# A two-layer vision network with selective scans, 16 images on one core: the order of instructions written by hand in place of a scheduler's

## The chip, the cores and the metric

The kernel runs on one core of a Trainium2 chip. The metric is the time of one execution on the device, in microseconds (us); less is better. The core has a matrix engine (PE, with its weight loads shown apart as PEld), a vector engine (DVE), an activation engine (ACT), a general engine (POOL), and SP, which here only issues DMAs. Each takes the instructions of its own queue in the order in which the program holds them; between engines they wait on semaphores.

## The reference, cut to what matters

Sixteen images of 48 x 48 pixels and 96 channels pass through two layers. Each layer adds a convolution-and-scan block and then a feed-forward block. The scan block is what costs:

```python
xz = x @ in_proj_w.T; xc, z = split(xz)             # 192 channels each
xc = silu(depthwise_conv3x3(xc))
xs = 4 directions of xc                             # rows, columns, both reversed
dts, B, C = split(x_proj(xs))                       # 6 + 16 + 16 per direction
delta = softplus(dt_proj(dts) + bias)
h = h * exp(delta * A) + (delta * u) * B            # 2304 pixels, 192 channels, 16 states
y = sum over states of h * C                        # + Ds * xs
y = merge of the 4 directions, then * silu(z)
out = y @ out_proj_w.T
```

The first layer also has a branch on y: a product to 384 channels, a 3 x 3 depthwise convolution, a product to 96, scaled by a squeeze-and-excite factor. The second normalizes y over its channels ahead of the gate. The feed-forward block multiplies values rounded to 8-bit floats and rounds sums to 16 bits.

## The kernel before, in words

**Scan steps.** One image and layer is 288 scan steps (`STEPS`): two pairs of directions, three chunks of 768 pixels (`CH`), three groups j of 128 channel-direction rows, four parts i of 32 channels, four groups g of 4 states. The 128 partitions are 32 channels x 4 states. A step is: ACT computes `a = exp(d * rate)` into one of two PSUM buffers (line 484); POOL multiplies `b = du * B` (line 486); DVE runs the recurrence along the pixels (`tensor_tensor_scan`, line 518); the result is multiplied by C into `hc` (line 520), by DVE in place of `a` for three steps of four, and by POOL from a buffer of its own `h` for the fourth (`SHARE`); ACT copies the last column as carry for the next chunk (line 522); PE sums the 4 states with a constant matrix into the PSUM tile `py` (the fold, line 524, two products of 384 columns). `py` starts with the skip term or the first pair's result (line 504), and after 16 steps ACT copies it out (line 533) and it is stored (line 534). There are four buffers of `b` and of `hc`, four of `d` (delta and delta*u, a DMA for every four steps, line 466) and six of `bc` (B and C, four DMAs for every 24 steps, line 475).

**The other work** is written as generators that yield weights: `first` (norm, projection, convolution, and the inputs of the scan of layer 0), `middle` (all between the scan of layer 0 and that of layer 1 of one image: merge of directions, gate, `branch`, out-projection, feed-forward, then `before` for layer 1) and `final` (merge, `centred`, gate, out-projection, feed-forward). `conv` (line 324) makes a depthwise convolution of nine products by diagonal matrices per 384 pixels (line 333). Products go to two PSUM buffers (`pst`) and are evicted by ACT or DVE. `before` ends with the dt stage: for six column blocks, products (line 430), an eviction with bias (line 431), a softplus over 2304 pixels (line 435), and three products `du` on POOL (line 442).

**Phases.** `together` (line 781) runs one scan, 288 steps, and lets the other image's generators go on by weight, so that they end at 94% of the scan (`AHEAD`). For images in pairs the phases are: layer 0 of m beside `final(m-1)` and `first(m+1)`; layer 0 of m+1 beside `middle(m)`; layer 1 of m beside `middle(m+1)`; layer 1 of m+1 beside `final(m)` and `first(m+2)`. That is 32 phases. `first(0)` runs ahead of them and `final(15)` behind.

**What sets the order.** The program is traced in this order, but the framework's scheduler then orders each engine's instructions by priority and by buffers that come free. So the order on an engine isn't quite that of the text: the built program has, for instance, two scans ahead of two products in many places, and merges that start earlier than written. DMAs are issued by SP (loads, `du`) and by ACT (`y`, `u`, `dd`, `bc`, `xt` stores).

Of the kernel before, what the change touches and what calls it, by code (L numbers as in the profile page):

```python
# [13 lines left out]
BF16 = mybir.dt.bfloat16  # L14
F8 = mybir.dt.float8e5
AF = mybir.ActivationFunctionType
ALU = mybir.AluOpType
# [120 lines left out]
class Net:  # L138
    def __init__(self, ctx, tc, wpack, at, b2, ffw):
# [11 lines left out]
        self.xp = pool("xp", bufs=1)  # L151
        self.big = pool("big", bufs=5)
# [105 lines left out]
        self.turn = 0  # L258
# [12 lines left out]

    def norm(self, x, eps):

        nc = self.nc
        m = self.small.tile([128, NT], F32, name="m")
        nc.vector.tensor_reduce(m, x, AX.X, ALU.add)
        nc.vector.tensor_scalar_mul(m, m, 1.0 / DM)
        xm = self.bigt([128, NT, DM], "xm")
        nc.gpsimd.tensor_tensor(xm, x, m.unsqueeze(2).broadcast_to([128, NT, DM]), ALU.subtract)
        yield 6  # L280
        sq = self.bigt([128, NT, DM], "sq")
        nc.scalar.activation(sq, xm, AF.Square)
        s = self.small.tile([128, NT], F32, name="s")
        nc.vector.tensor_reduce(s, sq, AX.X, ALU.add)
        yield 2
        nc.scalar.activation(s, s, AF.Sqrt, bias=self.eps[eps], scale=1.0 / DM)
        r = self.small.tile([128, NT], F32, name="r")
        nc.vector.reciprocal(r, s)
        nc.gpsimd.tensor_tensor(xm, xm, r.unsqueeze(2).broadcast_to([128, NT, DM]), ALU.mult)
        yield 4  # L290
        return xm

    def channels_first(self, xn, dt, name):
# [3 lines left out]
        for q in range(NQ):  # L297
            p = self.pst()
            for i in range(TQ):
                nc.tensor.transpose(p[:DM, i * 128 : (i + 1) * 128], xn[:, TQ * q + i, :], self.ident)  # L300
            out = xt[:, q * SUB : (q + 1) * SUB]
# [4 lines left out]
            yield 1  # L306
# [17 lines left out]
    def conv(self, p, name, done):  # L324

        nc = self.nc
        dg = self.one.tile([128, 9, 128], F32, name="dg")
        nc.sync.dma_start(dg.rearrange("p k m -> p (k m)"), self.taps[name])
        for q in range(NQ):
# [10 lines left out]
            yield 6  # L340
            done(q, o)
            yield 0.8
# [3 lines left out]
    def before(self, t, s, x):  # L346
# [4 lines left out]
        nc.scalar.dma_start(s["xt"], xt)  # L351
        u = [None] * 3
        cb = self.get(t + "cb")
        for name, half in (("wxa", "a"), ("wxb", "b")):
            p = self.padded(name)
            for q in range(NQ):
                o = self.pst()
                nc.tensor.matmul(
                    o[:, :SUB], lhsT=self.get(t + name), rhs=xt[:, q * SUB : (q + 1) * SUB], start=True, stop=True
                )  # L360
                nc.scalar.copy(self.inside(p, q), img(o[:, :SUB]))
                yield 0.7
            if half == "a":
                u[0] = self.bigt([128, L], "u0")

                def done(q, o):
# [4 lines left out]
                yield from self.conv(p, t + half, done)  # L371
                nc.scalar.activation(u[0], u[0], AF.Silu)
                yield 1
                u[1] = self.bigt([128, L], "u1")
                nc.scalar.copy(swapped(u[1][64:]), img(u[0][64:]))
                yield 1
                u[2] = self.bigt([128, L], "u2")
                nc.scalar.copy(swapped(u[2][:64]), img(u[0][:64]))
                nc.scalar.dma_start(s["u"][0], u[0])
                yield 1  # L380
            else:

                def done(q, o):
# [10 lines left out]
                yield from self.conv(p, t + half, done)  # L394
                nc.scalar.activation(u[1][:64], u[1][:64], AF.Silu)  # L395
                nc.scalar.activation(u[2][64:], u[2][64:], AF.Silu)
                yield 1
                for j in (1, 2):
                    nc.scalar.dma_start(s["u"][j], u[j])
# [5 lines left out]
        for c in range(NCH):  # L405
            row = self.work.tile([128, CH], F32, name="row", tag="w3")
            for q in range(2):
                cs = slice(c * CH + q * SUB, c * CH + (q + 1) * SUB)
                for w, m in ((wdt, 4 * DR), (wbc, 128)):
                    o = self.pst()  # L410
                    for j in range(3):
                        nc.tensor.matmul(  # L412
                            o[:m, :SUB], lhsT=w[:, j, :], rhs=u[j][:, cs], start=(j == 0), stop=(j == 2)
# [489 lines left out]
```

## Time and profile before

| | |
|---|---|
| median of 3 runs | 29325.72 us (29315.92 to 29372.79) |
| profiled execution | 29326.56 us |
| its span, first to last instruction | 29324.8 us |
| busy: PE, DVE, POOL, ACT | 82%, 80%, 79%, 48% |
| weight loads (PEld) | 43% |
| DMA | 150 GB/s mean, 4406 MB |
| mean granted PE clock | 0.898 |
| first scan starts | 203.1 us |
| last scan ends | 176.5 us before the end |

The page says for each group of instructions how long it was busy and what ended the idle time of its engine before it. The waits view sums the latter by pairs of waiter and releaser. The windows view gives each engine's busy time in chosen stretches. A PE that is shown busy isn't always at its peak, since matrix products are pipelined and their ends modelled; its granted clock is 1.00 or 0.50 at any time, and a mean in a stretch.

The scan lines in numbers: 9216 steps; the product on POOL (line 486) 1819 ns, the recurrence on DVE 1741 to 1813 ns, the product on DVE 947 ns, the exponential on ACT 906 ns.

### The profile page before, as it was taken

The page shows a single profiled execution, that of the slowest core. Times are in us where ns is not written, and L with a number is a line of the kernel's source. Part 1 is how long each engine was busy: PE and PEld are TensorE (multiplying, and loading weights), DVE is VectorE, ACT ScalarE, POOL GpSimd, SP SyncE. Part 2 cuts the span into 40 slices and gives each one's busy share as a digit, 9 for nine tenths or more (in the row PEclk, how much of TensorE's full clock was granted, in tenths as well). Part 3 has the DMA queues.
Part 4 walks back from the last instruction along what each step waited for, and adds up shares of the span by engine and source line. Part 5 has one row for each costly group of instructions (what it writes and reads, how often), then busy time and mean ns, then how long its engine had stood idle before and what let it go on. Part 6 is the DMA issues. An engine that isn't in the chain of part 4 may idle for free. (4 is left out here: it accounts for less than half of the span.)

```text
span 29324.8 us, 227106 instructions
## 1 busy us (share of the span) xinstructions
PE 24033.6 (82%) x68224; PEld 12726.8 (43%) x68224; DVE 23488.3 (80%) x18372; ACT 14074.7 (48%) x22093; POOL 23241.6 (79%) x13238
## 2 busy tenths in 40 slices
PE   7888878888788887888788887888778888788886
PEld 3444444444444444444444444444444444344443
DVE  6877888778887788877888778887788877888777
ACT  4454444544445454444444444444444444444443
POOL 6877788778887788877888778787787877877777
PEclk8988899989999899998999989999898998989988
DMA  4444444444444444444444444444444344443443
GB/s 155 153 156 152 146 148 155 154 151 149 148 152 154 154 152 148 148 156 149 159 143 151 151 149 160 144 148 153 150 164 145 141 154 150 162 148 143 150 156 109
DMA packets 1062581, 4406.37 MB, mean 150 GB/s; under 512 B 211936, under 2 KB 211936, under 8 KB 1030368
## 3 DMA queue, kind: packets, MB, share of 16 engines
q1 hardware_dynamic: 869792, 3757.78, 36.2%
q10 hardware_dynamic: 191552, 634.06, 5.5%
q8 instruction: 536, 8.78, 0.1%
q14 instruction: 701, 5.74, 0.1%
HBM read 3500.22 MB, written 891.22 MB: 150 GB/s over the span
## 5 line engine op out<-in xcount | busy, mean ns | idle before, releaser
L486 POOL TENSOR_TENSOR b<-d,bc 128x768 f32<-128x768 f32 x9216 | 16584.7, 1819 | 4084.2 <-DVE a L518 2783.7
L524 PE MATMUL py<-hc,fold_sb 128*128 128x384 f32 x36864 | 14564.0, 540 | 3265.9 <-DVE hc L520 1991.2
L524 PEld LDWEIGHTS py<-hc,fold_sb 128*128 128x128 f32 x36864 | 7359.8, 208 | 9807.3 <-DVE hc L520 3050.8
L484 ACT ACTIVATE a<-d,l_a 128x768 f32<-128x768 f32 x9216 | 8304.2, 906 | 5248.7 <-DVE h L518 2817.0
L518 DVE TENSOR_TENSOR_SCAN a<-a,carry,b 128x768 f32<-128x768 f32 x4608 | 8252.7, 1813 | 2037.9 <-ACT a L484 1438.6
L520 DVE TENSOR_TENSOR hc<-a,bc 128x768 f32<-128x768 f32 x6912 | 6427.8, 947 | 1034.1 <-PE py L524 873.5
L520 POOL TENSOR_TENSOR hc<-h,bc 128x768 f32<-128x768 f32 x2304 | 4187.6, 1818 | 1511.8 <-DVE h L518 1115.4
L518 DVE TENSOR_TENSOR_SCAN a<-a,b 128x768 f32<-128x768 f32 x2304 | 4002.9, 1755 | 1091.6 <-ACT a L484 612.1
L522 ACT COPY carry<-a 128x1 f32<-128x1 f32 x4608 | 725.2, 158 | 5229.7 <-DVE hc L520 5210.7
L518 DVE TENSOR_TENSOR_SCAN h<-a,carry,b 128x768 f32<-128x768 f32 x1536 | 2766.9, 1801 | 484.0 <-ACT a L484 354.4
L333 PE MATMUL pst<-e,dg 128*128 128x384 f32 x5184 | 1730.3, 486 | 0.0
L430 PE MATMUL pst<-dts,wpack_sb 24*128 24x384 f32 x2304 | 1200.8, 636 | 513.9 <-ACT dl L431 434.2
L518 DVE TENSOR_TENSOR_SCAN h<-a,b 128x768 f32<-128x768 f32 x768 | 1337.2, 1741 | 303.9 <-POOL b L486 236.0
L333 PEld LDWEIGHTS pst<-e,dg 128*128 128x128 f32 x5184 | 977.2, 189 | 705.5 <-PE py L524 25.5
L333 PE MATMUL pst<-wxa,dg 128*128 128x384 f32 x3456 | 1173.3, 492 | 24.9 <-DMA dg<-taps_l0a 20.0
L442 POOL TENSOR_TENSOR du<-dl,u 128x768 f32<-128x768 f32 x576 | 1033.6, 1809 | 201.2 <-DMA dd<-du 100.4
L333 PE MATMUL pst<-wxb,dg 128*128 128x384 f32 x3456 | 1169.7, 489 | 5.6 <-issue 5.6
L431 ACT ACTIVATE dl<-pst,wpack_sb 128x384 f32<-128x384 f32 x1152 | 644.0, 577 | 1072.5 <-PE pst L430 581.4
L430 PEld LDWEIGHTS pst<-dts,wpack_sb 24*128 24x128 f32 x2304 | 446.7, 223 | 1206.6 <-ACT dl L431 661.4
L504 PE MATMUL py<-first,ident 128*128 128x384 f32 x1152 | 570.7, 629 | 484.5 <-ACT yt L533 479.6
L412 PE MATMUL pst<-u,wpack_sb 128*24 128x384 f32 (+1 forms) x2304 | 831.7, 492 | 65.2 <-ACT u L395 23.0
L333 PEld LDWEIGHTS pst<-wxa,dg 128*128 128x128 f32 x3456 | 661.5, 192 | 509.4 <-issue 44.6
(143 smaller groups left out, 15283.5 us busy)
## 6 DMA issues: line engine op xcount, KB each, us to landing
d<-dd SPq DMA_DIRECT2D x2304, 768.0 KB, 4.6
bc<-bc SPq DMA_DIRECT2D x1536, 768.0 KB, 6.0
dd<-dl ACTq DMA_DIRECT2D x192, 1152.0 KB, 4.7
dd<-du SPq DMA_DIRECT2D x576, 384.0 KB, 2.5
y<-yt ACTq DMA_DIRECT2D x576, 384.0 KB, 3.1
u<-u ACTq DMA_DIRECT2D x96, 1152.0 KB, 5.1
first<-u SPq DMA_DIRECT2D x288, 384.0 KB, 3.3
first<-y SPq DMA_DIRECT2D x288, 384.0 KB, 3.1
```

The costliest lines, as they stand in the source:

```text
L333: nc.tensor.matmul(img(o[:, :SUB]), lhsT=dg[:, k, :], rhs=img(p, PW)[:, PQ * q + i : PQ * q + i + PQ, j : j + HW], start=(k == 0), stop=(k ...
L412: nc.tensor.matmul(o[:m, :SUB], lhsT=w[:, j, :], rhs=u[j][:, cs], start=(j == 0), stop=(j == 2))
L430: nc.tensor.matmul(o[:, :SUB], lhsT=dtw[:, col, :], rhs=dts[:, cs], start=True, stop=True)
L431: nc.scalar.activation(dl[:, cs], o[:, :SUB], AF.Identity, bias=self.get(t + "dtb")[:, col : col + 1])
L442: nc.gpsimd.tensor_tensor(du, dl[:, cs], u[j][:, cs], ALU.mult)
L484: nc.scalar.activation(a, d[:, 0, :], AF.Exp, scale=rates[:, pair, j, i, g : g + 1])
L486: nc.gpsimd.tensor_tensor(b, d[:, 1, :], bc[:, 0, :], ALU.mult)
L504: nc.tensor.matmul(py[:, q, :SUB], lhsT=self.skip[t][:, j, :] if pair == 0 else self.ident, rhs=first[:, q * SUB : (q + 1) * SUB], start=True,
L518: nc.vector.tensor_tensor_scan(way(h), way(a), way(b), start, ALU.mult, ALU.add)
L520: (nc.vector if here else nc.gpsimd).tensor_tensor(hc, h, cc, ALU.mult)
L522: nc.scalar.copy(carry[:, at : at + 1], h[:, last : last + 1])
L524: nc.tensor.matmul(py[:, q, :SUB], lhsT=self.fold[:, i, :], rhs=hc[:, q * SUB : (q + 1) * SUB], start=False, stop=((i, g) == (3, GROUPS - 1)),
```

## The change

The whole traced part is put into `manual_schedule`, so each engine takes its instructions in the order of the text, and the text is rewritten for that:

- All 32 scans become one loop over 9216 steps (`scans`). In turn n it writes: due loads of `bc` and `d` (three tiles of four steps ahead); the recurrence of step n, the product on DVE if it is DVE's, the carry copy; the exponential of step n+2; POOL's product b of step n+3; POOL's product hc of step n, if it is POOL's; the fold of step n-1 (of n-2, if POOL made its hc); then pieces of the other work.
- The other work is cut into smaller pieces. `piped` runs products and their evictions as stages, an eviction one piece behind its product; `columns` and `conv` use it. Whole-image POOL instructions of norms and merges are split into thirds, and large ACT instructions are followed by larger yields.
- Weights are set anew: 320, 720 and 244 for `first`, `middle` and `final`, in place of 201, 464 and 151; the other work ends after 268 of 288 steps. In a `middle` phase the weights of the parts are 25 for the merge, 47 gate, 189 branch, 20 squeeze, 32 out-projection, 91 feed-forward, 46 norm and turn, 118 projection and convolution, 26 x-projection, 126 dt stage; in `final` 25, 39.4 (`centred`), 47, 42, 91.
- All stores go from ACT's queue to SP's. The pool of large buffers has six in place of five and now holds the tokens `xs`, the branch's `tm` (whole image) and the feed-forward's 8-bit tile.

The work itself, in count and size of instructions, is otherwise the same. The diff, cut to its core:

```diff
+    def piped(self, n, weight, *stages):
+        vals = [None] * n
+        for t in range(n + len(stages) - 1):
+            for k in reversed(range(len(stages))):
+                q = t - k
+                if 0 <= q < n:
+                    r = stages[k](q, vals[q])
+                    if inspect.isgenerator(r):
+                        r = yield from r
+                    vals[q] = r
+            yield weight if t < n else 1
...
-    def conv(self, p, name, done):
...
+    def conv(self, p, dg, put):
+        nc = self.nc
+        def nine(q, _):
             o = self.pst()
             for k in range(9):
...
-            yield 6
-            done(q, o)
-            yield 0.8
+                if k in (1, 3, 5):
+                    yield 1.5
+            return o
+        yield from self.piped(NQ, 2, nine, put)
...
+        def inputs(pair, j, dl):
+            to = s["dd"][pair, j].rearrange("p (c w f) -> p c w f", c=NCH, w=2)
+            nc.sync.dma_start(to[:, :, 0, :], dl.rearrange("p (c f) -> p c f", c=NCH))
+            for c in range(NCH):
+                du = self.work.tile([128, CH], F32, name="du", tag="w3")
+                cs = slice(c * CH, (c + 1) * CH)
+                nc.gpsimd.tensor_tensor(du, dl[:, cs], u[j][:, cs], ALU.mult)
+                nc.sync.dma_start(to[:, c, 1, :], du)
+                yield 2
...
+                yield from self.columns(1.5, put, (dtw[:, col, :], dts))
                 nc.scalar.activation(dl, dl, AF.Softplus)
-                to = s["dd"][pair, j].rearrange("p (c w f) -> p c w f", c=NCH, w=2)
-                nc.scalar.dma_start(to[:, :, 0, :], dl.rearrange("p (c f) -> p c f", c=NCH))
-                yield 1
...
+                yield 5
+                if done:
+                    yield from inputs(*done)
+                done = pair, j, dl
+        yield from inputs(*done)
...
+            if here:
+                product()
+                product = None
+            if c != (NCH - 1, 0)[pair]:
+                nc.scalar.copy(kept["carry"][:, at : at + 1], h[:, last : last + 1])
+            folds.append((n + (1 if here else 2), n, hc))
+            return product
...
+            for g, slot in enumerate((-16, -16, -3, -2)):
+                bc_at[block * 6 * GROUPS + slot if block else -16].append((block, g))
+        load_first(0)
+        for n in range(-4 * GROUPS, len(steps) + 3):
+            for block, g in bc_at.get(n, ()):
+                load_bc(block, g)
+            if n % GROUPS == 0 and 0 <= n // GROUPS + 3 < tiles:
+                load_d(n // GROUPS + 3)
+            product = step(n) if 0 <= n < len(steps) else None
+            if 0 <= n + 2 < len(steps):
+                decays(n + 2)
+            if 0 <= n + 3 < len(steps):
+                added(n + 3)
+            if product:
+                product()
+            while folds and folds[0][0] <= n:
+                _, m, hc = folds.popleft()
+                folded(m, hc)
+            if 0 <= n < len(steps):
+                f = n // STEPS
+                share = (n % STEPS + 1) / (AHEAD * STEPS)
+                while todo[f] is not None and (given[f] < total[f] * share or share >= 1):
+                    w = next(todo[f], None)
+                    if w is None:
+                        todo[f] = None
+                    else:
+                        given[f] += w
...
+        low = self.bigt([64, L], "low")
+        nc.scalar.copy(img(low), swapped(y[2][64:]))
+        yield 4
+        third = HW // 3
+        for into, of in ((img(y[0][:64]), swapped(y[2][:64])), (img(y[0][64:]), swapped(y[1][64:]))):
+            for i in range(3):
+                at = slice(i * third, (i + 1) * third)
+                nc.gpsimd.tensor_tensor(into[:, at], into[:, at], of[:, at], ALU.add)
+                yield 2
...
-WORK = {"first": 201, "middle": 464, "final": 151}
-AHEAD = 0.94
+WORK = {"first": 320, "middle": 720, "final": 244}
+AHEAD = 268 / 288
...
+    with tc.manual_schedule():
+        for _ in first(0)[0]:
+            pass
+        net.scans(phases)
+        for _ in final(NB - 1)[0]:
+            pass
```

## The prediction

> **What bounds the kernel now.** I read the page first, then cut the span at every 288th scan (line 518), since one phase of the program is 288 scan steps with the other image's work beside them. The columns of the two rows below: window, length, then busy time of PE, PE weight load, DVE, ACT, POOL (with instruction counts), granted PE clock, DMA share, GB/s. The first row is a phase with `middle` beside the scan, the second one with `final` and `first`.
>
> ```profile
> 11936.10:12876.20 940.10, 803.10 (x2290) 426.66 (x2289) 734.63 (x565) 450.59 (x706) 727.92 (x419) 0.90 0.41 147
> 13814.60:14694.40 879.80, 696.21 (x1981) 369.40 (x1980) 732.58 (x581) 429.62 (x675) 725.01 (x410) 0.90 0.44 156
> ```
>
> DVE and POOL are each 78% busy in the first and 83% in the second: three engines carry nearly the same load and none is full on average. Phases of one kind repeat within a few us: 16 with `middle` at about 938, 14 of the other kind at about 880, the first phase (only `first` beside it) 829.5, the last (only `final`) 782.8; 203.0 us lie ahead of the first scan and 176.5 behind the last. So the stage decides. I cut the `middle` phase where lines begin and end: merge and gate; branch convolutions; squeeze and out-projection; norms and feed-forward; the next layer's convolutions; x-projection (line 412); dt stage (lines 430 to 444); scan alone.
>
> ```profile
> 11936.10:12025.10 89.00, 66.86 (x169) 32.00 (x167) 64.44 (x49) 48.97 (x77) 81.83 (x46) 0.87 0.46 167
> 12025.10:12280.10 255.00, 253.81 (x772) 143.04 (x772) 212.96 (x164) 113.87 (x200) 195.68 (x116) 1.00 0.36 128
> 12280.10:12333.10 53.00, 49.97 (x183) 32.88 (x181) 42.63 (x37) 17.48 (x21) 33.79 (x20) 0.84 0.35 126
> 12333.10:12471.10 138.00, 92.22 (x288) 46.42 (x288) 121.53 (x107) 61.98 (x106) 110.72 (x68) 0.85 0.36 122
> 12471.10:12647.10 176.00, 153.17 (x450) 87.77 (x449) 130.19 (x95) 85.17 (x143) 122.33 (x71) 0.92 0.38 137
> 12647.10:12703.10 56.00, 49.93 (x144) 21.98 (x142) 40.04 (x30) 30.18 (x52) 35.81 (x20) 1.00 0.34 128
> 12703.10:12837.10 134.00, 110.13 (x228) 49.06 (x229) 87.29 (x64) 79.45 (x95) 108.81 (x62) 0.78 0.59 220
> 12837.10:12876.10 39.00, 26.90 (x65) 13.46 (x64) 35.44 (x26) 13.48 (x16) 38.84 (x20) 0.78 0.43 157
> ```
>
> The branch stage is PE-bound (253.8 of 255.0 us, clock 1.00); merge and gate are POOL-bound; feed-forward is DVE's; the dt stage has no full engine, its time is waits. Line 518 alone, over the same cuts, gives 28, 86, 15, 39, 55, 17, 37, 15 scans (one at a cut counts twice). The waits (waiter <- releaser: total us, times, longest) say who is late for DVE:
>
> ```profile
> DVE a L518 <- ACT a L484: 2050.8, 1411, 13.0
> DVE a L518 <- ACT carry L522: 905.8, 859, 11.3
> DVE hc L520 <- PE py L524: 873.5, 695, 5.7
> POOL b L486 <- DMA bc<-bc: 815.6, 471, 5.4
> ```
>
> ACT is 48% busy and yet it is the usual releaser: its exponentials stand behind evictions that wait for PE and behind long activations. The timeline of DVE near the last scans shows what a step costs there:
>
> ```profile
> 28901.04 1.75 DVE L518 TENSOR_TENSOR_SCAN a<-a,b 128x768 f32<-128x768 f32 x1
> 28902.90 0.96 DVE L520 TENSOR_TENSOR hc<-a,bc 128x768 f32<-128x768 f32 x1
> 28903.78 1.75 DVE L518 TENSOR_TENSOR_SCAN a<-a,b 128x768 f32<-128x768 f32 x1
> 28911.65 1.80 DVE L520 TENSOR_TENSOR hc<-a,bc 128x768 f32<-128x768 f32 x2
> 28913.81 1.82 DVE L518 TENSOR_TENSOR_SCAN a<-a,carry,b 128x768 f32<-128x768 f32 x1 [0.36 <-ACT carry L522]
> ```
>
> A product that follows its own scan starts 1.86 us after it; the next scan 0.88 later: 2.74 per pair. In the order scan, scan, product, product starts follow at some 1.7 and 0.86, but the exponential of the next step, which needs the product's PSUM buffer, then comes 0.36 late.
>
> **What the Trainium skill says.** "PSUM — Partial Sum Buffer", Engine vs sequencer instructions: ScalarE, VectorE and GpSimd queues are strict FIFO. The trace agrees: exponentials idle behind other lines' waits. "VectorE: DVE Perf Modes", The DRAIN you can't avoid: each DVE instruction waits for the pipe to empty, and a semaphore costs nothing extra. Here it does: 1.86 us from scan to dependent product, about 1.7 to an independent instruction; I use the trace. "ScalarE: Activation LUTs", What ACT_TABLE_LOAD costs: about 1283 ns; the trace has 1283 ns. "TensorE: Matmul & The Clock Gate", Part 1: the array runs at half or full clock, by recent activity. The trace agrees (granted clock 1.00 in the branch stage, 0.78 in the dt stage), so a denser PE needn't be priced at 0.90.
>
> **The change, part by part.** The instructions are the same but for small splits (norms in thirds, merge adds in parts), so what moves is order. The built order shows it: scan and product alternate, exponentials two steps ahead, POOL's product three, folds one or two behind.
>
> *Step cost on DVE.* Three steps of four become 2.74, the fourth (product on POOL) about 1.72: 9.94/4 = 2.48 us. The waits for the exponential go, since a pair lies between; after a POOL step only 1.7 lies between against 0.06 + 0.16 + 0.91 + 0.1 = 1.25 of carry copy and exponential, both from the trace. So 288 steps are 715 us, plus 30 to 40 of other DVE work. Light stretches gain little: line 518 alone has 81 scans in the 200 us from 28900, one at a cut counted twice: about 2.5 a step already.
>
> *Pacing.* New weights: `middle` is 720 over 268 steps, 2.69 a step, and 20 steps stay alone. Steps per stage are weight/2.69. PE takes 0.329 us per record (253.8/772), so 0.658 per 384-column product and 1.32 per step of folds. POOL takes 1.78 per instruction back to back (rows of four: 7.12), so 1.25 x 1.78 = 2.23 a step. Each stage takes the largest of the three:
> - merge and gate, 72 -> 26.8 steps: POOL 26.8 x 2.23 + 17.4 + 10.7 = 88, less 7 for its lead of three steps, plus 12 for waits. The `low` copy now stands on ACT ahead of later exponentials, behind fold 1.3, copy 0.8, y write 3.1 (its landing) and a load of 1152 KB (5.1, as u's): 93.
> - branch, 189 -> 70.3 steps: PE 216 x 0.658 + 70.3 x 1.32 + 6 = 240. Before it had 86 steps and 255 us: the convolution's share of weight falls from 44% to 28%, so it is squeezed into fewer steps.
> - squeeze and out-projection, 52 -> 19.4: 58.
> - norms and feed-forward, 137 -> 51: DVE 51 x 2.48 + 31 = 157.
> - next convolutions, 118 -> 43.9: 110 (PE, 30 steps) + 18 + 17 + 5 for SiLU and its table loads = 150.
> - x-projection, 26 -> 9.7: PE 23.7 + 12.8 = 36.5.
> - dt stage, 126 -> 46.9: POOL 46.9 x 2.23 + 18 x 1.78 = 137, less its lead, plus a few us of softplus with its two table loads (2.13 + 2.57): 140.
> - scan alone, 20: 49.5.
>
> Sum 924; plus 7 for bc loads whose buffer comes free three steps ahead of use (landing takes 6.0 us, two POOL products hide 3.6): 931 against 940, -9. Bounds: POOL's lead hides the bc and y waits, -20; none is hidden, +25.
>
> For `final` with `first` (564/268 = 2.1 a step) the same way: merge (POOL 11.9 x 2.23 + 17.4, +1), centring (DVE 18.7 x 2.48 + 6, +2) and gate (POOL 22.3 x 2.23 + 10.7, +3) 162; out-projections (20 steps) 58; feed-forward (43.2) 136; norm and turn (23.7) 65; convolutions (38 steps PE-bound at 121, 18 of DVE's at 44, +5) 170; x-projection (12.3) 40; dt stage (POOL 59.8 x 2.23 + 32, less a little lead) 164; alone 49.5. Sum 845, plus 7 for bc, plus 4 for the load of the tokens: 856 against 880, -24 (-45 to 0). The first phase (320/268) is DVE-bound: 715 + 10 + some 25 for ACT and POOL = 750, -80. The last: 715 + 45 + 11 = 771, -12.
>
> *Ahead and behind.* The written order puts the seven tap tables (DVE until 53 us) ahead of the first norm, which the scheduler began at 17.9, and the first scan behind all of `first`: from 203 to about 248, +45 (10 to 70). The tail is one image without scans in both: 0.
>
> *Buffers.* A sixth big buffer, with the tokens and the feed-forward's fp8 tile in it, changes no instruction; 476 us of ACT waiting for POOL's `du` (line 431 on 442) should go with it and is part of the dt stage above. *DMAs.* All issues of ACT's queue go to SP's (y, u, dd, bc, xt). ACT loses some 0.3 us each, on 960 issues, mostly in idle time: nothing counted. SP now waits in order for yt, rows and products; behind it stand d loads (12 steps ahead, 30 us: hidden) and bc loads (2 to 3 steps ahead: the 7 us above).
>
> Sum: 16 x -9 = -144; 14 x -24 = -336; -80; -12; +45: -527. The profiled execution has 29326.56 us, its span 29324.8, the median is 29325.72, one time for this purpose: 28,800 us, -1.8%.
>
> **Rivals.** *The waits hide too:* the DVE-bound and POOL-bound stages lose nothing beside their loads: 27 a `middle` phase and 25 the other kind less, 782: 28,020. For: the last scan-only stretches have DVE 95% busy. Against: softplus, SiLU and copies of 2 to 4 us hold the exponentials in any order. *PE falls short in the squeezed stretches (slower):* the folds and evictions share in-order queues with it, and the convolution stage of before had PE busy 153.2 of 176.0 us, 87%. PE-bound time after is some 440 us of a `middle` phase and 215 of the other; at 87% that is 66 and 32 more: 1500 in all, 30,300. It turns the sign once PE is busy below about 95% there (527/1500 of 13 points). For it: only two PSUM buffers for products. Against: the branch stage ran at 99.5%. *No change:* gains cancel within 0.2%, about what a measurement of this kernel can tell from none: 29,325. That the order isn't taken as written is excluded by the built order.
>
> **Chances.** Forecast 0.47 (own range 28,300 to 29,250), hidden waits 0.16, short PE 0.29, cancelled 0.08. Faster 0.63, same 0.08, slower 0.29. The range leaves out the best of the first rival and the worst of the second: 27,900 to 29,900.
>
> **What would show it.** Right: about 931 and 856 us a phase; PE near 99% and clock 1.00 in the branch stage at 3.4 us a step; scan to product at 1.86 throughout; DVE's waits for ACT down from some 3450 us to under 1500, those for PE up from 870; first scan near 250. Wrong: phases of both kinds below 850, or PE with idle time in the convolution stages while DVE waits for ACT.

## The result: slower by 2.4%, and the profile after

The median of four runs is 30049.29 us (30041.38 to 30060.83); four runs of the kernel before beside them have 29330.68 us. The ratio is 1.0243, with a 95% interval of 1.0225 to 1.0261. The profiled execution has a span of 30052.5 us, 727.7 more than before. Cut at every 288th scan (line 627 now), it falls into:

| | forecast, us | measured, us | difference to before, all |
|---|---|---|---|
| until the first scan | +45 | 260.1 (203.1) | +57 |
| first phase | -80 | 756.6 (829.3) | -73 |
| 16 `middle` phases, each | -9 | 974.6 (937.1) | +600 |
| 14 of the other kind, each | -24 | 890.7 (881.4) | +130 |
| last phase | -12 | 792.7 (782.8) | +10 |
| behind the last scan | 0 | 179.3 (176.5) | +3 |

The sign turns in the repeated phases. Here is the `middle` phase from 12201.0 us, cut as the one before was (window, length, busy time of PE, PE weight load, DVE, ACT, POOL, granted clock, DMA share, GB/s): merge and gate; branch convolutions; squeeze and out-projection; norms and feed-forward; next convolutions; x-projection; dt stage; scan alone.

```profile
12201.00:12301.90 100.90, 59.17 (x145) 29.09 (x146) 68.78 (x51) 46.61 (x76) 88.55 (x50) 0.80 0.45 163
12301.90:12537.40 235.50, 233.57 (x697) 128.82 (x697) 164.15 (x121) 93.47 (x178) 154.21 (x95) 0.99 0.32 113
12537.40:12614.50 77.10, 66.41 (x227) 39.89 (x226) 65.01 (x55) 26.33 (x32) 50.76 (x29) 0.87 0.32 105
12614.50:12787.00 172.50, 110.77 (x328) 56.60 (x327) 156.17 (x130) 71.45 (x115) 132.05 (x87) 0.81 0.33 117
12787.00:12938.00 151.00, 142.87 (x428) 81.17 (x426) 103.69 (x75) 77.66 (x125) 100.87 (x62) 0.98 0.36 129
12938.00:12981.00 43.00, 38.28 (x110) 17.37 (x110) 28.77 (x20) 21.31 (x40) 25.06 (x14) 0.96 0.44 165
12981.00:13129.00 148.00, 115.59 (x276) 55.62 (x275) 118.43 (x84) 92.89 (x124) 130.87 (x74) 0.85 0.61 213
13129.00:13175.20 46.20, 32.55 (x80) 16.79 (x80) 43.47 (x33) 16.09 (x18) 44.71 (x26) 0.85 0.50 183
```

Forecast were 93, 240, 58, 157, 150, 36.5, 140, 49.5. The two convolution stages (second and fifth line) came as forecast, PE 99% and 95% busy: 386.5 us against 390. They hold 66 and 43 scans; before they had 86 and 55 in 431 us. Some 32 steps were pushed out of the stages in which a step costs least (PE's four fold products, so (431 - 386.5)/32 = 1.39 us) into the others. Those took 587.7 us for 179 steps, before 509.1 for 147: 2.46 us for each step more. 32 x (2.46 - 1.39) = 34 us, which is the whole difference of these two phases (974.2 - 940.1). It must be, since both prices are differences divided by the same 32 steps; whether the squeeze is the cause, the first experiment asks. Put otherwise: at the 2.48 us of a bare step on DVE, the other stages hold 509.1 - 147 x 2.48 = 144.5 us beyond the scan before, and 587.7 - 179 x 2.48 = 143.8 after. At this price the written order took nothing off that. The forecast had (931 - 390) - 174 x 2.48 = 110.

The waits of after (waiter <- releaser: total us, times, longest) say why:

```profile
DVE a L627 <- ACT carry L637: 2504.8, 643, 14.5
...
ACT tm L743 <- PE pst L394: 1238.2, 288, 7.2
DVE a L627 <- ACT a L574: 857.3, 494, 5.9
...
ACT yt L612 <- PE py L603: 819.0, 283, 7.4
...
ACT u L429 <- PE pst L394: 719.3, 156, 28.7
```

The view says that the scans wait less for exponentials (857.3 us, before 2050.8) and more for the carry copy (2504.8, before 905.8). The names mislead here. A scan reads a carry of the chunk before, written 48 steps earlier; of ACT it needs only its own exponential. In the trace of after, the 762 scans that wait by name for the carry (`a` and `h` together) start 0.10 us behind the end of their own exponential, as the other 568 do; the carry copy merely ends in between. So both are one wait, for the exponential. Over all scans it was 3447 us in 2549 waits before, and is 3737 us in 1330 waits after: half as many, 2.8 us each in place of 1.35. ACT itself now stands for PE at every one of the 288 branch evictions (`tm`, 1238.2 us against 497.7). Over all lines ACT waits 5006 us for PE, before 3372. The timeline of ACT and DVE in the branch stage shows one such wait (start, length, engine, line, ..., idle time before it):

```profile
12329.54 1.75 DVE L627 TENSOR_TENSOR_SCAN a<-a,b 128x768 f32<-128x768 f32 x1
12331.62 0.96 DVE L631 TENSOR_TENSOR hc<-a,bc 128x768 f32<-128x768 f32 x1 [0.33 <-PE py L603]
12334.85 0.67 ACT L743 ACTIVATE tm<-pst,bn_b,bn_s 128x384 f32<-128x384 f32 x1 [7.24 <-PE pst L394]
12335.42 0.15 ACT L637 COPY carry<-a 128x1 f32<-128x1 f32 x1
12335.60 0.91 ACT L574 ACTIVATE a<-d,l_a 128x768 f32<-128x768 f32 x1
12336.44 0.15 ACT L637 COPY carry<-a 128x1 f32<-128x1 f32 x1
12336.60 1.77 DVE L627 TENSOR_TENSOR_SCAN a<-a,b 128x768 f32<-128x768 f32 x1 [4.03 <-ACT carry L637]
```

ACT stands 7.24 us at the eviction, until PE has the piece. The exponential at 12335.60 is that of the scan at 12336.60. Nothing on DVE holds it later than the first scan shown, but it stands behind the eviction, and so its scan stands 4.03 us. PE has work throughout: it isn't late by waiting, it is full.

### The profile page after: what moved, and what is told of

Its sections match the earlier page's. It is cut to its first block, busy times and chain, and to the rows that moved or that the text cites. A ratio compares the mean times of both kernels' runs of the same rounds, so it can differ in the third digit from the quotient of the medians.

```text
span 30052.5 us, 228448 instructions
## 1 busy us (share of the span) xinstructions
PE 23943.1 (80%) x68224; PEld 12686.2 (42%) x68224; DVE 23984.3 (80%) x18372; ACT 13991.5 (47%) x22020; POOL 23233.8 (77%) x13686
## 5 line engine op out<-in xcount | busy, mean ns | idle before, releaser
L580 POOL TENSOR_TENSOR b<-d,bc 128x768 f32<-128x768 f32 x9216 | 16542.7, 1812 | 3999.2 <-DVE a L627 3547.8
L603 PE MATMUL py<-hc,fold_sb 128*128 128x384 f32 x36864 | 15024.3, 550 | 4460.1 <-POOL hc L631 2229.8
L603 PEld LDWEIGHTS py<-hc,fold_sb 128*128 128x128 f32 x36864 | 7477.7, 212 | 11449.6 <-DVE hc L631 3263.9
L627 DVE TENSOR_TENSOR_SCAN a<-a,carry,b 128x768 f32<-128x768 f32 x4608 | 8359.8, 1814 | 1955.5 <-ACT carry L637 1158.3
L631 DVE TENSOR_TENSOR hc<-a,bc 128x768 f32<-128x768 f32 x6912 | 6622.0, 958 | 679.5 <-PE py L603 22.7
L627 DVE TENSOR_TENSOR_SCAN h<-a,carry,b 128x768 f32<-128x768 f32 x1536 | 2777.4, 1808 | 285.5 <-ACT carry L637 133.0
L295 PE MATMUL pst<-dts,wpack_sb 24*128 24x384 f32 x2304 | 1081.8, 581 | 192.5 <-ACT dl L505 191.3
L394 PEld LDWEIGHTS pst<-wxb,dg 128*128 128x128 f32 x3456 | 656.1, 190 | 464.8 <-issue 6.9
L612 ACT COPY yt<-py 128x768 f32<-128x768 f32 x576 | 457.7, 795 | 821.9 <-PE py L603 819.0
L295 PE MATMUL pst<-u,wpack_sb 128*128 128x384 f32 (+1 forms) x2304 | 816.3, 499 | 8.4 <-ACT u L458 4.5
```

The source lines that it names most:

```text
L295: nc.tensor.matmul(o[: w.shape[1], :SUB], lhsT=w, rhs=y[:, q * SUB : (q + 1) * SUB], start=(k == 0), stop=(k == len(terms) - 1),)
L394: nc.tensor.matmul(img(o[:, :SUB]), lhsT=dg[:, k, :], rhs=img(p, PW)[:, PQ * q + i : PQ * q + i + PQ, j : j + HW], start=(k == 0), stop=(k ...
L580: nc.gpsimd.tensor_tensor(b, d[:, 1, :], bc[:, 0, :], ALU.mult)
L603: nc.tensor.matmul(py[:, q, :SUB], lhsT=self.fold[:, i, :], rhs=hc[:, q * SUB : (q + 1) * SUB], start=False, stop=end,)
L612: nc.scalar.copy(sub(yt), py[:, :, :SUB])
L627: nc.vector.tensor_tensor_scan(way(h), way(a), way(b), start, ALU.mult, ALU.add)
```

## The experiments

Ratios are to the kernel before, run on the same chip. For the runs that bear on the stages, this table has the mean of the 16 `middle` phases, worked out from the trace: the two stretches from the first to the last convolution product, and the rest, with their scans. The last column is the rest less 2.48 us a scan. That is the price when each product stands directly behind its own scan. Under the scheduler, the kernel before included, most don't, and a scan costs less; in e2 this can make up some 20 us of the column.

| | ratio | convolutions: us, scans | rest: us, scans | beyond 2.48 |
|---|---|---|---|---|
| before | 1 | 419.5, 137 | 517.6, 151 | 143 |
| after | 1.0243 | 354.4, 98 | 620.2, 190 | 149 |
| e1, convolution weights doubled | 1.0065 | 404.9, 134 | 539.6, 154 | 158 |
| e2, under the scheduler | 0.9802 | 348.4, 106 | 568.2, 182 | 117 |
| e7, scheduler, weights doubled | 0.9897 | 431.7, 137 | 503.1, 151 | 129 |
| e16, e1 without waits at evictions | 0.9788 | 401.0, 133 | 518.6, 155 | 134 |
| e17, after without them | 1.0057 | 341.2, 97 | 617.0, 191 | 142 |
| e18, e2 without them | 0.9711 | 395.5, 122 | 513.5, 166 | 103 |

### The squeezed convolutions

```diff
                 if k in (1, 3, 5):
-                    yield 1.5
+                    yield 3
             return o
-        yield from self.piped(NQ, 2, nine, put)
+        yield from self.piped(NQ, 4, nine, put)
-WORK = {"first": 320, "middle": 720, "final": 244}
+WORK = {"first": 398, "middle": 915, "final": 244}
```

> The changed kernel with every weight of the convolution doubled (and the totals with it), so that a convolution gets about 3.9 steps per 384 pixels in a middle phase in place of 2.4; the kernel before had 4.0. Theory 1 (the new weights squeeze the PE-bound convolutions into too few scan steps; each step pushed out of them costs a full DVE step of 2.5 to 3.3 us elsewhere and saves only 1.3 us of PE): some 44 steps go back in a middle phase and fewer in the others, the middle phases fall from 975 to about 925 us, the whole to 28,900 to 29,200 us. Theory 2 (the loss is waits at the head of in-order queues: the copy low behind the y loads, exponentials behind evictions): the phases stay within 10 us of the changed kernel, 29,900 to 30,100 us.

e1: 29521.36 us, 1.0065 (1.005 to 1.008): 1.8 of the 2.4 points come back, less than hoped. The convolution stretches have 36 scans more and 50.5 us more (1.40 each), the rest 80.6 less (2.24 each). So in the written order the squeeze is shown as a cause, at its size: 527 us between the two spans, 16 x 30 of them in the `middle` phases. The part beyond the scan does not fall with it (149 us, now 158).

### The written order itself

```diff
-    with tc.manual_schedule():
+    if True:
```

> The changed kernel's text with the manual schedule taken off, so that the framework's scheduler orders each engine's instructions again. Theory 1: the weights still squeeze the convolutions, but the scheduler can move work across: near the changed kernel or a little better, 29,500 to 30,100 us. Theory 2: the in-order waits go, and the time falls below the kernel before, under 29,300 us. Theory 3 (the written order of the steps is the better one and only hidden by the rest): over 30,200 us.

e2: 28750.77 us, 0.9802 (0.9787 to 0.9816): the new text, without the written order, is faster than both kernels, and the fastest version here that computes the reference. It is squeezed too (106 scans beside the convolutions), and still has 32 us a phase less beyond the scan. With the weights of the first run on top:

> The changed text under the scheduler (0.9802 of the kernel before in its run) with the doubled convolution weights as well. If the squeeze of the convolutions into too few scan steps costs there what it costs in the written order (0.018), the ratio is 0.962 to 0.972. If the scheduler, which takes what is ready, already spreads TensorE's work, it stays within 0.975 to 0.985.

e7: 29035.97 us, 0.9897 (0.9882 to 0.9911), slower than with its own. From the first scan to the end of the last, the written order takes 1244 us more than the scheduler with the kernel's own weights (29613.1 and 28368.7), and 423 us more with the doubled ones (29084.0 and 28661.1). Under the scheduler the doubled weights add 83 us to the convolutions for 31 scans, 2.7 each, twice their price in the written order. Weights are not a property of the work alone; they fit one order.

What does the scheduler do better? The waits of ACT for PE at three evictions, in e1 (written order):

```profile
ACT tm L743 <- PE pst L394: 748.2, 256, 4.9
...
ACT dl L505 <- PE pst L295: 543.8, 366, 5.7
...
ACT u L429 <- PE pst L394: 335.0, 86, 28.3
```

and in e2 (scheduler):

```profile
ACT dl L505 <- PE pst L295: 422.9, 288, 6.3
...
ACT tm L743 <- PE pst L394: 132.4, 128, 3.0
...
ACT u L429 <- PE pst L394: 90.5, 38, 28.7
```

Also, only 1354 of its 6912 DVE products stand directly behind their own scan (1535 in the kernel before). In the written order all do. There a product starts 1.84 to 1.93 us after its scan, where an instruction that does not read it mostly follows a scan after 1.65 to 1.73. At some 0.185 us each that is 0.185 x (6912 - 1354) = 1030 us of DVE time. Two candidates, then: evictions, and dependent products. The sum of the scans' waits for ACT does not part the orders: 3158 us in e1, 3331 in e2.

### Single waits taken away, one at a time

The `low` copy behind its y load (382.2 us of ACT's waits), with a wider gap between (`yield 10` ahead of the copy):

> The changed kernel with a yield of 10 between the y loads of a merge and the ACT copy low that waits for them (totals of middle and final raised by 10). Theory 2: the 382 us in which ACT waits for these loads, and most of the 417 us in which DVE stands still around that copy, go: 29,600 to 29,700 us. Theory 1 alone: no more than 100 us.

e3: 30028.09 us, 1.0237: nothing. Of the wait, 109.6 us are left, but the wait of `tm` rose from 1238.2 to 1394.0 and that of `u` from 719.3 to 826.2. The stores back on ACT's queue (`nc.sync.dma_start` to `nc.scalar.dma_start` for xt, u, rows, dd, y):

> The changed kernel with the stores of the working data (xt, u, B and C rows, dd, y) put back on ScalarE's queue, as the kernel before has them. If the move of these stores to SyncE's queue delays the loads behind them and so the scans (POOL waits for the B and C tiles 371 us in all), it gains up to 300 us, ratio 1.013 to 1.024. If a store on ScalarE's queue holds up the exponentials behind it until its data is ready, it loses 100 us and more, ratio above 1.027. If neither matters, it is within 0.3% of 1.0243.

e8: 30117.23 us, 1.0266 (1.025 to 1.0281): not the cause; its interval and that of 1.0243 overlap. With the doubled weights, convolution evictions half a piece later, in the middle of the next piece:

> The changed kernel with the doubled convolution weights of the second experiment run (1.5 to 3 after each part, 2 to 4 after each piece, sums 398/915/244), and in addition each convolution's eviction is written in the middle of the next piece instead of at its beginning, so that TensorE may lag about three scan steps before ScalarE stands still for it. If ScalarE waiting for a lagging TensorE, with exponentials and carries behind it, is what is left (the eviction and fold waits of the run with doubled weights are about 750 + 335 + 240 us), the ratio to the kernel before falls from 1.0065 to 0.985 to 0.998. If those waits are only a symptom of TensorE being the bound of that stretch, it stays within 0.2% of 1.0065.

e5: 29468.24 us, 1.005: the wait of `tm` fell from 748.2 to 467.9 us, and the time by 0.15 points, within the intervals. With two PSUM buffers for the pieces an eviction can't stand much later. Folds one or two steps later, so that PE doesn't stand for POOL's products (here the merge loads y before the last steps of the phase before are stored, so that block's values are older ones; the instructions are the same):

```diff
-            hc = self.sw.tile([128, CH], F32, name="hc", bufs=4)
+            hc = self.sw.tile([128, CH], F32, name="hc", bufs=6)
-            folds.append((n + (1 if here else 2), n, hc))
+            folds.append((n + (2 if here else 4), n, hc))
```

> The changed kernel with the doubled convolution weights (1.0065), and every fold one or two steps later: two steps behind a product of VectorE (one before), four behind a product of POOL (two before), with six hc buffers in place of four. In the second run TensorE stands 2188 + 1790 us (weight loads and matmuls) for products of POOL, and what is written behind those folds, the convolutions and projections, stands too; ScalarE's evictions then come late, and the exponentials and carries behind them. If that chain is what the written order loses, TensorE's waits for POOL fall under 1000 us, VectorE's waits for ScalarE (1596 + 1150 us) fall by a third or more, and the time falls by 300 to 900 us, a ratio of 0.976 to 0.996. If TensorE's waits are slack, only they fall and the ratio stays within 0.3% of 1.0065.

e11: 29585.3 us, 1.0082. PE's waits for POOL's products at the fold fell from 2188.1 + 1790.3 (e1: weight loads, matmuls) to 1586.1 + 1352.2 us only, and nothing was gained.

### The dependent product

To put a product behind the next scan needs a third `a`. It was put in SBUF (with one buffer of `h` in place of two):

```diff
-            a = self.ps.tile([128, 2, 512], F32, name="a", tag="ps").rearrange("p q f -> p (q f)")[:, :CH]
+            a = self.sw.tile([128, CH], F32, name="a", bufs=3)
```

> The changed kernel with the decay tile a in three SBUF buffers in place of two PSUM buffers (and one buffer of h in place of two). It asks two things: whether DVE is slower or faster with a in SBUF (control for a later order of the products), and whether the exponential's lead of two PSUM buffers is a limit. Theory 2: with one more buffer and no PSUM bank shared between the carry copy and the product, DVE's waits for the carry (2505 us) shrink: 29,000 to 29,600 us if the instruction times stay. Theory 1: within 200 us of the changed kernel, since the convolutions stay PE-bound. If recurrence or product take longer from SBUF, the time rises by 9216 times the difference in light stretches.

e4: 43467.1 us, 1.4818: no test of the order, but of where `a` lies; see the last section. So the order was changed with `a` in PSUM, and with the doubled weights: scan, scan, scan, product, product, scan, product.

```diff
             product = step(n) if 0 <= n < len(steps) else None
-            if 0 <= n + 2 < len(steps):
+            if product and n % 4 == 1:
+                kept["product"], product = product, None
+            elif product and n % 4 == 2:
+                kept["product"]()
+                decays(n + 1)
+                product()
+                product = None
+            if 0 <= n + 2 < len(steps) and (n < 0 or n % 4 != 1):
                 decays(n + 2)
```

> The changed kernel with the doubled convolution weights, and in each four steps the product of the second is written after the scan of the third (scan, scan, scan, product, product, scan, product), so that two of the three products on VectorE no longer stand directly behind the scan that they read. If the 0.185 us that a dependent product costs (1.86 against 1.67 us from scan to next instruction) is on the path, it gains 0.185 x 2 x 2304 = 850 us less what the third exponential's shorter cover costs (0.905 us plus two signals against one product of 0.87 us, at most 0.25 us x 2304 = 580 us): 270 to 850 us, a ratio of 0.978 to 0.997. If ScalarE's queue eats it, as the rival has it, the ratio is 1.00 to 1.03.

e6: 29489.93 us, 1.0053 (1.0038 to 1.0068): no gain. A new wait had come, DVE's product for ACT's carry copy, though both only read `a`:

```profile
DVE hc L631 <- ACT carry L637: 1824.0, 717, 15.4
```

With the copy written behind the product:

> The pair order of the sixth run with the doubled convolution weights, and each of its carry copies written behind the product that reads the same PSUM tile, as the changed kernel has it. In the sixth run the carry copy stood ahead of the product, and VectorE's product waited for ScalarE's copy, though both only read the tile: 1824 us in 717 waits. If that is where the gain of the pair order went, 1824 less the 716 us by which the waits of the scan for the carry had fallen, some 1100 us, come back in part: 28,500 to 29,150 us, a ratio of 0.972 to 0.994. If the written order loses the time to ScalarE's queue whatever stands there, the wait moves to the next scan's exponential or carry and the ratio stays within 0.3% of 1.0053.

e9: 29591.55 us, 1.0088 (1.0071 to 1.0105). That wait is gone, and it stands elsewhere, as the expectation's second case said (both lines are the wait for the scan's exponential):

```profile
DVE a L627 <- ACT carry L639: 2344.4, 1336, 15.0
...
DVE a L627 <- ACT a L574: 1667.3, 1206, 6.7
```

DVE is busy 23465.4 us in place of 23932.0, and stands longer for ACT by more: 4268 us in place of 3355 over all lines. With the kernel's own weights, and with the later folds:

> The changed kernel with its own weights, and the pair order with the carry copy behind its product. If the dependent product and the squeeze of the convolutions are two separate losses, the gain over the changed kernel (1.0243) is the same as that of the run beside it over the doubled weights (1.0065). If the pair order gains nothing, it stays within 0.3% of 1.0243.

> As the run beside it, with the pair order of the ninth run (1.0088 without the later folds). The pair order saves 0.185 us of VectorE time on two thirds of its products but leaves ScalarE less room; if late evictions took that room, it now gains on the run beside it, by up to 600 us. If the exponential's shorter cover itself is what ate it, it is again the same as the run beside it within 0.3%.

e10: 30133.07 us, 1.0271, against 1.0243; and e12: 30045.88 us, 1.0237, against 1.0082. In e10 DVE is busy 23488.1 us, as in the kernel before (23488.3), and the kernel is some 800 us longer. As long as ACT's waits stand, the dependent product isn't on the path in the written order. What it costs on DVE is cover for ACT, and taking it away exposes ACT. Without those waits the pair order was not run.

### ACT standing for PE

Evictions two pieces behind need a third PSUM buffer for pieces. To make room for it, the two decay tiles, each 2 x 512 columns for 768 used ones, were packed as halves of one tile of 3 x 512:

```diff
-            a = self.ps.tile([128, 2, 512], F32, name="a", tag="ps").rearrange("p q f -> p (q f)")[:, :CH]
+            a = both[:, n % 2 * CH : (n % 2 + 1) * CH]
```

> The changed kernel with the doubled convolution weights (1.0065), with the two decay tiles packed into three PSUM banks, so that the pieces of the other image's work have three PSUM buffers in place of two, and nothing else. The evictions stand in ScalarE's queue where they stood, so if ScalarE's wait for a late TensorE is what holds the scans, this alone changes little: ratio 1.002 to 1.009. If TensorE's waits for evictions (438 + 198 us and the like) count, it gains 100 to 300 us. It can lose if the packing lets ScalarE write and VectorE read one bank at a time and that slows either: then the exponential takes over 0.93 us or the scan over 1.84 us.

> As the run beside it, and every eviction is written two pieces behind its matmuls in place of one, which the third buffer allows (sums of the weights 411/943/252). If ScalarE standing at evictions for a TensorE that is late (1734 us at projections and 1322 us at convolutions in the second run) holds back the exponentials and carries behind them, those waits fall to a third, VectorE's waits for ScalarE (some 3100 us) fall by 500 us or more, and the ratio is 0.975 to 0.995. If those waits only stand where another would, the ratio stays within 0.3% of the run beside it.

> The changed text under the scheduler with its own weights (0.9802), with three PSUM buffers for the pieces as in the two runs beside it. A third buffer lets the scheduler put more between a piece and its eviction: 0.970 to 0.980 if evictions hold the scans there too, within 0.3% of 0.9802 if not.

e13 to e15: 37460.2, 37548.74 and 39301.34 us (1.2771, 1.2801, 1.3396). One tile meant one dependence. In e13, over nine recurrences in ten start 0.10 us behind the end of the exponential of the step after it, which writes the other half of the tile; their own had ended some 4.2 us before they start. And that exponential needs the product of the step ahead of the recurrence. The timeline of e13:

```profile
12001.23 0.96 DVE L632 TENSOR_TENSOR hc<-a,bc 128x768 f32<-128x768 f32 x1
...
12002.27 0.16 ACT L638 COPY carry<-a 128x1 f32<-128x1 f32 x1 [3.02 <-DVE hc L632]
12002.47 0.91 ACT L575 ACTIVATE a<-d,l_a 128x768 f32<-128x768 f32 x1
12003.47 1.77 DVE L628 TENSOR_TENSOR_SCAN a<-a,b 128x768 f32<-128x768 f32 x1 [1.29 <-ACT a L575]
```

Carry, exponential and two signals stand between the product and the next scan, 1.29 us a step. These runs say what it costs when recurrence and exponential can't overlap (37460 - 29521 = 7940 us, e13 against e1), and nothing on evictions. So the wait itself was taken away. ACT's evictions read a constant, and the other image's values are left out:

```diff
-                nc.scalar.copy(self.inside(p, q), img(o[:, :SUB]))
+                nc.scalar.copy(self.inside(p, q), img(self.still[:, :SUB]))
...
-                        o[:, :SUB],
+                        self.still[:, :SUB],
```

> The changed kernel with the doubled convolution weights (1.0065), in which every eviction of a piece on ScalarE reads a constant SBUF tile of the same shape instead of the piece's PSUM tile: the other image's values are constants, TensorE still does every matmul, ScalarE still does every eviction in the same place of its queue, but never stands for TensorE there (it stood 1734 + 1322 us, 3100 of its 3880 us of waits for TensorE). If ScalarE standing behind a late TensorE is what the written order loses over the scheduler, VectorE's waits for ScalarE (3355 us) fall by 1000 us or more and the ratio is 0.96 to 0.985. If something else holds the scans, the ratio is over 0.995.

> The same constant in place of the pieces' PSUM tiles in the changed kernel with its own weights (1.0243). ScalarE stands 5006 us for TensorE there. If the squeezed convolutions cost their time by this wait, the ratio falls to the neighbourhood of the run beside it, 0.965 to 0.99. If they cost it because TensorE itself is the bound of those stretches and hands its folds back late, more than 0.01 of the distance between the two runs stays.

> The control: the same constant in the changed text under the scheduler (0.9802), where ScalarE stands 2305 us for TensorE. If that wait costs the scheduler's order little, because what is ready goes ahead, it gains at most 0.01: 0.970 to 0.982. If it gains as much as the written order does, the wait is no reason for the difference between the two orders.

e16 to e18: 28706.55 us (0.9788, 0.9771 to 0.9804), 29495.89 us (1.0057, 1.0042 to 1.0072) and 28484.74 us (0.9711, 0.9696 to 0.9725). In e16, the waits for ACT of the scans that write `a`, under both names:

```profile
DVE a L629 <- ACT carry L639: 958.9, 208, 14.5
...
DVE a L629 <- ACT a L576: 581.1, 251, 6.9
```

1540 us where e1, with the same weights, had 1149.7 + 1595.8 = 2745. PE is as busy, 99% between the first and the last product of the branch convolutions. A part of these gains lies ahead of the first scan, so compare from the first scan to the end of the last:

| | with the waits, us | without, us | gain |
|---|---|---|---|
| written order, own weights (after, e17) | 29613.1 | 29135.6 | 478 |
| written order, doubled weights (e1, e16) | 29084.0 | 28347.3 | 737 |
| scheduler, own weights (e2, e18) | 28368.7 | 28203.8 | 165 |

So the wait is a cause in the written order, at 478 or 737 us, and costs the scheduler less. The gains include PE's own waits for those evictions, which the constant takes away too; the runs don't part the two. How much of the distance between the two orders goes with it depends on the weights. Each order at the better of its two weights (e1 and e2), it is 572 of 715 us. With the kernel's own weights in both it is 313 of 1244 us, and 932 stay. For the doubled weights in both there is no run of the scheduler without the waits.

The squeeze does not go with the wait: 529 us lie between the two sets of weights with it, 788 without. The wait only changes its place, since PE is the bound of those stretches. In e17 DVE's product meets the late PE itself, where it waited 22.7 us in after (1123 us of this line lie in the convolution stretches):

```profile
DVE hc L633 <- PE py L605: 1298.1, 740, 4.0
```

What the 932 us are was not tested. The dependent products are large enough to be a candidate: all 6912 stand behind their own scan in e17, 907 in e18, an estimate of 0.185 x 6005 = 1110 us of DVE time.

## Why the prediction was wrong

- *"PE 216 x 0.658 + 70.3 x 1.32 + 6 = 240", and 150 for the next convolutions:* right, 235.5 and 151.0, PE 99% and 95% busy. The squeeze was seen, and its cost was in the sum, but too low: 41 us saved in the convolutions (431 to 390) against 32 more elsewhere (509 to 541) for 27 steps, 1.2 us each. A step that leaves the convolutions saves 1.4 us there and cost 2.2 to 2.5 elsewhere; what hid this is the next point.
- *"The waits for the exponential go, since a pair lies between":* this is the step that failed. The pair covers an exponential that ACT has begun, not one behind an eviction for which ACT stands up to 7 us. The scans' waits for their exponentials, forecast to fall from some 3450 us to under 1500, are 3737 us: half as many, each twice as long. With them, the 34 us forecast to vanish from the rest of a `middle` phase (144 to 110) stayed. So it is in the other kind: the stages outside its convolutions hold 143 us beyond the scan, before 131 (mean of the 14 phases). Taking ACT's waits for PE at evictions away gives back 478 us with the kernel's own weights (e17), PE's waits for these evictions included.
- *"those for PE up from 870":* the wrong way. DVE's product waits 22.7 us for PE after; the late PE is met by ACT first.
- *First phase -80, head +45:* right, -73 and +57. *Scan to product at 1.86 throughout:* right, 1.84 to 1.93. *DMAs at nothing:* right as far as the stores go, 0.2 points with overlapping intervals (e8); the issues are 992, not 960. *The `low` copy 93:* 100.9, but moving it gained nothing.
- *"PE falls short in the squeezed stretches (slower)", 30,300:* near in time (30,049), by another way. It priced PE as 87% busy in those stretches. PE was full there, and it was being full that held ACT. Its sentence "the folds and evictions share in-order queues with it" names the link that e16 and e17 bear out; the price was put on the wrong engine.

Left open: what keeps the two orders 932 us apart with the kernel's own weights when ACT doesn't wait at evictions; how much of the gain of e16 and e17 is ACT's wait and how much PE's; what the kernel before would gain without its own 3372 us of ACT's waits for PE; and why late folds and the pair order together cost 1.5 points.

## What to carry to other kernels

In a written order, ask of every instruction that waits for another engine what stands behind it on its own queue: an eviction that stands up to 7 us for a full engine holds everything that is ready, and a scheduler that lets ready work pass may be worth more than the spacing one writes. When weights spread side work over a main loop, price the move of one loop step from stage to stage as an exchange (here 1.4 us against 2.2 to 2.5). A sum of waits in a trace isn't a gain: of those taken away here none gave its sum, and several came back at the next instruction of the queue. And the name that a view gives to a wait is that of the last signal before its end; check it against what the instruction reads.

## What the runs showed of the hardware

With `a` in SBUF (e4) the recurrence and the products of both engines slow each other. Groups of that run: line, engine, operation, count, busy us, mean ns.

```profile
L579 POOL TENSOR_TENSOR b<-d,bc 128x768 f32<-128x768 f32 x9216 | 23971.1, 2617 | 3582.0 <-DVE a L626 3512.5 <-DMA bc<-bc 41.2 <-DMA d<-dd 15.5
L630 DVE TENSOR_TENSOR hc<-a,bc 128x768 f32<-128x768 f32 x6912 | 15772.2, 2282 | 669.2 <-DVE a L626 7.8 <-issue 2.7 <-PE pst L294 0.9
L626 DVE TENSOR_TENSOR_SCAN a<-a,carry,b 128x768 f32<-128x768 f32 x4608 | 13092.1, 2841 | 130.2 <-POOL b L579 81.0 <-ACT carry L636 49.1
L573 ACT ACTIVATE a<-d,l_a 128x768 f32<-128x768 f32 x9216 | 8590.5, 933 | 8879.6 <-DVE hc L630 7792.1 <-DVE h L626 877.1 <-issue 181.6
```

With `a` in PSUM the same rows have 1812, 958, 1814 and 904 ns. The Trainium skill, "GPSIMD Engine Reference", 1. Specifications, says that POOL shares SBUF interfaces with DVE and contends with DVE instructions that have two SBUF inputs. The run agrees: both slow down, the exponential on ACT hardly. It is the company of POOL and not SBUF itself: of the scans in the third line, the 293 with POOL busy for less than a tenth of their time took 1808 ns on average, and the 2424 with POOL busy for over nine tenths 3193; of the products, in the same way, 39 took 959 ns and 5389 took 2207. The PSUM that `a` takes buys the difference.
